# A hand-set order for the last layer's opening, attention stacks kept across layers, and a 128-row circuit network

## The chip, the cores and the metric

The kernel runs on one core of a Trainium2 chip. The core has five engines with queues of their own: TensorE (PE, matrix products, with weight loads shown as PEld), VectorE (DVE), ScalarE (ACT), GpSimd (POOL) and SyncE (SP, which here only issues DMAs). The metric is the device time in microseconds (us); smaller is better.

## What is computed

The input x has 2 batches of 1024 tokens with 128 features, in f32: 2048 tokens, worked as 16 tiles of 128 or 4 groups of 512 (groups 0 and 1 are the first batch). Four layers follow each other, each in this form:

```python
xn = layernorm(x)
x = x + attn(xn) * silu(ffn(xn))
```

- Layer 0: differential attention with 8 heads, and a ternary feed-forward network.
- Layer 1: attention in a window with 16 heads of 8, and 8 experts of which each token takes one.
- Layer 2: a "circuit": x1 = layernorm(xn + cumprod(cos(xn)) per head), q = cumprod(cos(first 16 features of x1)), then layernorm(x1 + W2 relu(W1 q + b1) + b2) with W1 512 x 16. As its ffn, 16 experts that each choose 256 tokens, beside one shared expert.
- Layer 3: causal attention with 16 heads of 8; as its ffn one linear layer whose 128 x 128 weight is rounded to 4 bits, plus a product of rank 16 (LoRA): xn Wq + (xn A) B + bias.

## The kernel before

x, xn, its transpose xnT and s (one of the two factors of the gating) stay in on-chip memory. The layers run one after the other.

**Attention of layers 1 and 3** is in the class `Heads`. `project_in(j)` makes the q and k products of one group (L527), splits each into three bf16 parts whose sum is the f32 number (`split3`, L464 to L467), and stores these to `parts` in DRAM (L541); then it makes the values into v (L548, L555). Heads are taken in fours, n = 0 to 7 (n // 4 is the batch). `loading_stacks(n)` gathers the parts of four heads as rows: a stack `ks` (L568) and a stack `qs` (L575), 12 DMAs on SP, in three buffers each (n % 3). Rows 72 to 127 of each stack are filled from a `blank` in DRAM (L512), once per layer, and v is set to ones (L501); in row 96 and on, q gets the negated row maxima (`maxima_rows`, L585 to L597), so that one product yields scores less their maximum.

In `l3_layer`, `maxima(n, c)` computes the scores of the c-th 512 tokens with 96 rows (sf L1674, sr L1689, with masks added by a product L1680) and reduces them on DVE (L1675, L1697). `attend(n, c)` computes them again transposed with 128 rows (st L1727), takes the exponential on ACT (L1736) and multiplies by v (o3p L647). `ahead(n)` loads stack n + 2 and makes the maxima of n + 1, and for n = 0, 1 projects groups 2 and 3. `Weave.run(main, side, a, b)` interleaves main with side, b steps of side to a steps of main; `later` defers a closure by some steps. In the loop over n only PE keeps the written order; in the opening none does, and the order of instructions is the scheduler's.

The opening runs: `enter` (layernorm and transposes; rs is made on POOL, L72) and `project_in` for groups 0 and 1, stacks 0, then groups 2 and 3, then `l3_ffn` for all groups (pz L1817, f3y L1822, and the 17-row LoRA and bias product L1823), then the maxima of n = 0, then the loop.

**Layer 2.** `Chosen.search` finds 16 thresholds in 15 rounds. `experts()` runs 97 steps, woven with `circuits()` and `forward()` (the circuit network). Per expert: weights (768 KB, L1574), gather of its tokens (POOL, L1536), transposes (L1541), f2g and f2u (L1497), gelu times product (L1499, L1501), f2y (L1583), scaling (L1593), and two scatters that add to `adds` in DRAM (POOL, L1556). `forward()` transposes q (L1445), makes h2p with 16 rows of contraction (L1454), relu (L1462), and y2p (L1470). At the end `adds` is fetched per group (L1630), passed through Silu (L1631) and gated into x on POOL (L148, L149).

Of the kernel before, what the change touches and what calls it, by code (L numbers as in the profile page):

```python
# [19 lines left out]
P = 128  # L20
# [26 lines left out]
BV = ("w3_s", "ln_g", "ln_b", "g1", "be1", "b2", "g2", "be2", "bv", "b2o")  # L47
WM = {}
for _n, _w in (
    ("qk1", 256), ("v1", 128), ("o1", 128), ("gate1", E1),  # L50
    ("w2_2", 512), ("gate2", E2), ("sh", 768),
    ("qk3", 256), ("v3", 128), ("o3", 128), ("kern", 128), ("lora_a", RANK),
):
    WM[_n] = (sum(w for _, w in WM.values()), _w)
# [88 lines left out]
def gate_residual(k, pool, t0, n, g, out=None, eng=None):  # L143
# [6 lines left out]
    if out is not None:  # L150
        nc.sync.dma_start(out[:, sl, :], k.x[:, sl, :])

# [260 lines left out]
def l0_ffn(k, wf):  # L413
    nc, tc = k.nc, k.tc
    w12, hw, w3 = wf
    with (
# [27 lines left out]
        for g in range(NG):  # L444
# [7 lines left out]
            y = tmp.tile([P, 4, D], F32, tag="y", name=f"f0y{g}")  # L452
# [8 lines left out]
def split3(k, pool, x, parts, n):  # L461

    nc = k.nc
    nc.scalar.copy(parts[0], x)  # L464
    nc.vector.tensor_tensor(x, x, parts[0], ALU.subtract)
    nc.scalar.copy(parts[1], x)
    nc.vector.tensor_tensor(parts[2], x, parts[1], ALU.subtract)  # L467


# [4 lines left out]
KD, KP, KM, KR = 72, 96, 99, P  # L474


class Heads:
# [5 lines left out]
    def __init__(self, k, ctx, weave, li, qk, v, o, bq=None, bk=None, bv=None, bo=None):  # L483
# [10 lines left out]
        self.dr = pool("d", 1, space=bass.MemoryType.DRAM)  # L494
        self.p_s, self.p_t, self.p_o = (pool("p" + n, c, space=PSUM) for n, c in (("s", 3), ("t", 3), ("o", 2)))

        self.ident_h = self.big.tile([P, P], BF16, tag="ident_h", name=f"ident_h{li}")
        nc.vector.tensor_copy(self.ident_h, k.ident)

        self.v = self.big.tile([P, NT, H1 * self.VW + 32], F32, tag="v", name=f"v{li}")  # L500
        nc.gpsimd.memset(self.v, 1.0)  # L501
# [5 lines left out]
        self.q, self.kk = [], []  # L507
        for j in range(3):
            q = self.big.tile([KR, 4, S], BF16, tag=f"qs{j}", name=f"qs{li}{j}")
            t = self.big.tile([KR, 4, S], BF16, tag=f"ks{j}", name=f"ks{li}{j}")  # L510
            for x in (t, q):
                nc.sync.dma_start(x[KD:P].rearrange("p h t -> p (h t)"), k.blank)  # L512
            self.q.append(q)
            self.kk.append(t)
        self.parts = [
            self.dr.tile([2, 3, P, S], BF16, tag=f"d{b}", name=f"parts{li}{b}") for b in range(B)
        ]

    def project_in(self, j):

        k, nc, u = self.k, self.k.nc, f"{self.li}{j}"
        b, c = divmod(j, 2)
# [1514 lines left out]
```

## Time and profile before

| what | value |
|---|---|
| runs before | 1928.09, 1928.19, 1936.4 us; median 1928.19 |
| profiled execution | 1931.13 us, span 1929.4 us, mean granted clock 0.926 |
| busy, share of the span | PE 88%, DVE 65%, ACT 44%, POOL 30% |

The stages in the profiled execution, by the span's clock:

| us | stage |
|---|---|
| 0 to 875 | layer 0's attention |
| 875 to 1036 | layer 0's feed-forward network |
| 1036 to 1087 | layer 1's opening, until its first exponentials |
| 1087 to 1285 | layer 1 |
| 1285 to 1388 | layer 2's opening, search and lists |
| 1388 to 1549 | layer 2's experts, until the last scatter is issued |
| 1549 to 1639 | last layer's opening |
| 1639 to 1929 | last layer's heads and the output |

A timeline line gives start, length, engine, line, operation, output <- inputs, shapes, how many, and in brackets the idle time before with what ended it. SPq is the issue of DMAs on SP's queue. The granted clock is 1 at full speed.

### The profile page before, as it was taken

The numbers are of one execution on the slowest core, as the hardware profiler recorded it, in microseconds if no ns is written. First come the engines' busy times: TensorE is split into PE (matmuls) and PEld (weight loads), VectorE is DVE, ScalarE is ACT, GpSimd is POOL, SyncE is SP. The second block draws the span as 40 slices with busy tenths as digits, with TensorE's granted clock in tenths as the row PEclk, the third lists the DMA queues.
The fourth block names the chain that finished last, engine by engine and source line by source line (L and its number), as shares of the span: only waits on it lengthen the run. The fifth ranks groups of instructions, "written<-read, shape, count | busy, mean of one in ns | idle before, by whom it ended". The sixth has DMA issues, their size and how long they took to land. (4 is left out here: it accounts for less than half of the span.)

```text
span 1929.4 us, 24564 instructions
## 1 busy us (share of the span) xinstructions
PE 1704.1 (88%) x7805; PEld 876.2 (45%) x7805; DVE 1255.6 (65%) x2572; ACT 845.4 (44%) x1850; POOL 571.9 (30%) x899
## 2 busy tenths in 40 slices
PE   4999999999999999989997698876589849999995
PEld 2344444444444444434445356444376724444442
DVE  3988888888878888863004454757671545887771
ACT  1555555555555555443114244342143330665564
POOL 2233333333334333330003622310164641102211
PEclk9999999999999999999998699986697965999998
DMA  6433333333424333330004554211042463112100
GB/s 193 100 89 84 89 81 101 84 93 78 101 71 105 79 88 81 74 87 0 1 0 100 123 144 125 65 61 27 24 127 70 95 136 54 43 43 56 32 2 12
DMA packets 111565, 145.58 MB, mean 75 GB/s; under 512 B 28019, under 2 KB 95740, under 8 KB 108204
## 3 DMA queue, kind: packets, MB, share of 16 engines
q1 hardware_dynamic: 85692, 93.12, 19.1%
q0 software_dynamic: 25456, 50.86, 10.8%
q8 instruction: 63, 1.03, 0.2%
q14 instruction: 66, 0.54, 0.1%
q10 hardware_dynamic: 288, 0.03, 0.0%
HBM read 60.22 MB, written 16.19 MB: 40 GB/s over the span
## 5 line engine op out<-in xcount | busy, mean ns | idle before, releaser
L281 PE MATMUL sc<-xnT,q 128*128 128x512 f32 x1024 | 506.2, 596 | 6.3 <-ACT e L293 6.3
L293 ACT ACTIVATE e<-sc,nm 128x1024 f32<-128x1024 f32 x256 | 285.2, 1114 | 350.2 <-DVE nm L291 267.5
L291 DVE TENSOR_REDUCE nm<-sc 128x1 f32<-128x1024 f32 x256 | 308.0, 1206 | 8.5 <-PE sc L281 8.4
L312 POOL DMA_DIRECT2D aT<-tT x384 | 205.0, 540 | 321.4 <-DVE tT L305 174.1
L281 PEld LDWEIGHTS sc<-xnT,q 128*128 128x128 f32 x1024 | 193.8, 191 | 234.3 <-issue 188.9
L323 PE MATMUL pz<-aT,xn 128*128 128x512 f32 x512 | 262.2, 596 | 4.8 <-DMA aT<-tT 4.8
L1736 ACT ACTIVATE e<-st 128x512 f32<-128x512 f32 (+3 forms) x384 | 166.2, 492 | 117.8 <-PE st L1727 111.8
L301 DVE SCALAR_TENSOR_TENSOR e<-e,c,e 128x1024 f32<-128x1024 f32 x128 | 164.1, 1282 | 3.3
L305 DVE STREAM_TRANSPOSE tT<-e 128x1024 f32<-128x1024 f32 x128 | 158.5, 1239 | 2.5 <-DMA aT<-tT 1.8
L323 PEld LDWEIGHTS pz<-aT,xn 128*128 128x128 f32 x512 | 97.9, 192 | 120.9 <-issue 112.0
L72 POOL TENSOR_TENSOR f<-fv,neg_half 128x1 f32<-128x1 f32 x128 | 83.8, 655 | 200.6 <-DVE fv L355 138.5
L1697 DVE TENSOR_REDUCE nm<-sr 128x1 f32<-128x384 f32 (+3 forms) x176 | 106.1, 637 | 38.1 <-PE sr L1689 37.6
L1727 PE MATMUL st<-qs,ks 128*128 128x512 bf16 (+3 forms) x384 | 116.2, 328 | 1.0 <-ACT e L1736 0.9
L341 PE MATMUL po<-vc,z 128*128 128x384 f32 x256 | 105.8, 495 | 5.8 <-ACT oc L352 2.2
L439 PE MATMUL f0h<-h,hw 128*128 128x512 f32 x256 | 110.0, 592 | 0.0
L1037 ACT ACTIVATE e<-st 128x384 f32<-128x384 f32 (+1 forms) x128 | 58.3, 476 | 115.9 <-PE st L1001 105.3
L1675 DVE TENSOR_REDUCE nf<-sf 128x1 f32<-128x512 f32 x128 | 82.2, 683 | 11.8 <-PE sf L1674 11.6
L647 PE MATMUL o3p<-e,v 128*32 128x512 f32 (+3 forms) x768 | 86.7, 498 | 0.0
L453 DVE TENSOR_TENSOR f0y<-f0o,bv 128x512 f32<-128x512 f32 x4 | 2.8, 692 | 121.3 <-PE f0o L449 121.3
L341 PEld LDWEIGHTS po<-vc,z 128*128 128x128 f32 x256 | 47.4, 191 | 72.8 <-issue 46.4
L439 PEld LDWEIGHTS f0h<-h,hw 128*128 128x128 f32 x256 | 48.6, 190 | 61.2 <-issue 61.2
L257 PE MATMUL pq<-xnT,m 128*128 128x512 f32 x128 | 69.6, 626 | 7.7 <-ACT oc L352 5.6
(381 smaller groups left out, 2606.3 us busy)
## 6 DMA issues: line engine op xcount, KB each, us to landing
aT<-tT SPq DMA_DIRECT2D x640, 64.0 KB
aT<-tT POOLq DMA_DIRECT2D x384, 64.0 KB
w<-in_l_e SPq DMA_DIRECT2D x16, 768.0 KB
qs<-parts SPq DMA_DIRECT2D x135, 64.0 KB
ks<-parts SPq DMA_DIRECT2D x45, 192.0 KB
parts<-hm SPq DMA_DIRECT2D x16, 384.0 KB
w<-in_l_w POOLq DMA_DIRECT2D x8, 640.0 KB
ks<-blank SPq DMA_DIRECT2D x6, 448.0 KB
```

The lines of the kernel that those rows point to most:

```text
L281: nc.tensor.matmul(ps[:, n * 512 : (n + 1) * 512], lhsT=q[:, m, hf * 512 + t * P : hf * 512 + (t + 1) * P], rhs=k.xnT[:, b * S + n * 512 : ...
L291: nc.vector.tensor_reduce(nm, ps, AX.X, ALU.max, negate=True)
L293: nc.scalar.activation(em, ps, AF.Exp, bias=nm, accum_out=(s1, s2)[m][:, t : t + 1])
L301: nc.vector.scalar_tensor_tensor(e[0], e[1], c, e[0], ALU.mult, ALU.add)
L305: nc.vector.transpose(tT[:, :, t % 2, :, :].rearrange("p j J c -> p J j c"), e[0].rearrange("p (J j a) -> p J j a", J=8, j=4),)
L312: (nc.gpsimd if j == 3 or (i == 0 and j > 0) else nc.sync).dma_start(aT[32 * j : 32 * j + 32, t - 1 : t + 1, i, :, :].rearrange("a t J c - ...
L323: nc.tensor.matmul(pz, lhsT=k.xn[:, 8 * b + J, :], rhs=st["aT"][:, :, :, J, :].rearrange("p t i c -> p (t i) c"), start=(J == 0), stop=(J ...
L341: nc.tensor.matmul(po.rearrange("p a d -> p (a d)"), lhsT=st["z"][:, t * P : (t + 1) * P], rhs=mats[h][1].rearrange("p a d -> p (a d)"), s ...
L439: nc.tensor.matmul(ph, lhsT=hw[:, l, c, j * P : (j + 1) * P], rhs=cur[:, c, cols], start=(c == 0), stop=(c == 3))
L1697: nc.vector.tensor_reduce(nm[:, tt, i0 : i0 + hb], ps, AX.X, ALU.max, negate=True)
L1727: nc.tensor.matmul(ps[:, n0:512], lhsT=kk[0:KR, i, kt * P : (kt + 1) * P], rhs=q[0:KR, i, c * 512 + n0 : c * 512 + 512], start=not diag, s ...
L1736: nc.scalar.activation(e[:, n0:512], ps[:, n0:512], AF.Exp)
```

## The change

- `Stacks` is made once, between layer 0's attention and its feed-forward network: the bf16 identity, v, the causal masks, the three pairs of stacks with their blank rows, and the parts in DRAM. Layers 1 and 3 share them. For layer 3 a stack is laid out as two halves of 512 tokens (`nc_` = 2), which can be loaded one by one.
- `project_in` is cut into `products`, `first_parts`, `split`, `store` and `project_values`. The first bf16 part is made straight from the product.
- Layer 3's opening is written out for PE, DVE, ACT, POOL and SP, and so is its loop: gating on DVE; groups 0 and 1; the first half of stack 0 on three queues; the maxima of the first 512 tokens; then attention for them, with the next maxima woven in. Groups 2 and 3 (`second_batch`) are woven into n = 1 and 2.
- Layer 3's rounded weight and its LoRA product are folded into one 128 x 128 matrix w3, in layer 2; the bias comes from a one-row product.
- The mask products of one tile in `maxima` become one.
- W1 of the circuit network is kept as four copies, padded with zeros to 128 rows; h2p takes 32 products of 256 columns for 16 of 512, in two halves.
- In the search, a step's candidate is made from a base prepared earlier.
- An expert's weights come in two DMAs (the f2y third behind the next expert's first part); some buffers are fewer (xg 3 for 4); the weave counts change.

```diff
+class Stacks:
...
+        nc.gpsimd.memset(self.v, 1.0)
...
+            for x in (t, q):
+                nc.sync.dma_start(x[KD:P], k.blank)
...
+        self.nc_, self.ct = (1, S) if li == 1 else (2, S // 2)
...
+            nc.scalar.activation(hm[:, 0, a, :], pq, **how)
+            if a == 1:
+                nc.scalar.activation(xf[:, 1, :], pq, **how)
+            elif bias is None:
+                nc.vector.tensor_scalar(xf[:, 0, :], pq, scale, None, ALU.mult)
+            else:
+                nc.vector.tensor_scalar(xf[:, 0, :], pq, scale, bias, ALU.mult, ALU.add)
...
+    def split(self, j):
+        nc = self.k.nc
+        xf, hm = self.hm[j]
+        for a in range(2):
+            nc.vector.tensor_tensor(xf[:, a, :], xf[:, a, :], hm[:, 0, a, :], ALU.subtract)
+            nc.scalar.copy(hm[:, 1, a, :], xf[:, a, :])
+        for a in range(2):
+            nc.vector.tensor_tensor(hm[:, 2, a, :], xf[:, a, :], hm[:, 1, a, :], ALU.subtract)
...
+            (nc.sync, eng or nc.sync)[a].dma_start(d[:, :, at : at + 512], self.hm[j][1][:, :, a, :])
...
-        eng, dma = (nc.vector, nc.sync) if self.li == 1 else (nc.gpsimd, nc.gpsimd)
+        eng, dma = (nc.vector, nc.sync) if self.li == 1 or n + c == 0 else (nc.gpsimd, nc.gpsimd)
...
+            if 0 < i < 14:
+                base = tile("base3", (P, 3), I32, bufs=2)
+                nc.vector.tensor_tensor(base, steps[:, i + 1, :], thr.to_broadcast([P, 3]), ALU.bitwise_or)
...
-                nc.vector.tensor_tensor(cand, steps[:, i + 1, :], thr.to_broadcast([P, 3]), ALU.bitwise_or)
+                nc.vector.tensor_tensor(cand, base, inc.to_broadcast([P, 3]), ALU.bitwise_or)
+        nc.vector.tensor_tensor(thr, thr, inc, ALU.bitwise_or)
...
+        w1 = pool.tile([P, 4, FF2], F32, tag="w1", name="w1_2")
+        nc.gpsimd.memset(w1, 0.0)
+        for i in range(4):
+            nc.gpsimd.dma_start(w1[32 * i : 32 * i + NQ, i, :], k.i["l2_w1"])
...
+            nc.tensor.matmul(pw, lhsT=k.lora[:, 0:P], rhs=k.lora[:, P:], start=True, stop=True)
+            nc.vector.tensor_tensor(k.w3, pw, wq, ALU.add)
...
-                    ph = [PS.tile([P, NG, P], F32, tag="y", name=f"h2p{i}_{j}") for i in (i0, i0 + 1)]
-                    for i in range(2):
-                        r = slice(32 * (i0 + i), 32 * (i0 + i) + NQ)
-                        nc.tensor.matmul(
-                            ph[i].rearrange("p n t -> p (n t)"),
-                            lhsT=k.w1_2[r, j * P : (j + 1) * P],
-                            rhs=qT[r, :, :].rearrange("p n t -> p (n t)"),
-                            start=True,
-                            stop=True,
-                        )
...
+                if n in (0, 2):
+                    h = gp.tile([P, 4, 4, 2, P], F32, tag="wide", name=f"h2{n}")
+                    for j in range(4):
+                        for i0 in (0, 2):
+                            ph = PS.tile([P, 2, 2, P], F32, tag="y", name=f"h2p{n}{i0}_{j}")
+                            for i in range(2):
+                                nc.tensor.matmul(
+                                    ph[:, i, :, :].rearrange("p n t -> p (n t)"),
+                                    lhsT=w1[:, i0 + i, j * P : (j + 1) * P],
+                                    rhs=qT[:, n : n + 2, :].rearrange("p n t -> p (n t)"),
+                                    start=True,
+                                    stop=True,
+                                )
+                            nc.scalar.activation(h[:, j, i0 : i0 + 2, :, :], ph, AF.Relu, bias=k.pv("b1", j))
+                            yield
...
-            weave.run(experts(), others, 1 + 6 * E2, 110)
...
+            weave.run(experts(), others, 1 + 6 * E2, 122)
...
-                    for i in range(hb):
-                        nc.tensor.matmul(
-                            ps[:, i, r - P : r],
-                            lhsT=hd.ident_h,
-                            rhs=mqk,
-                            start=(i == 0),
-                            stop=False,
-                            skip_group_check=True,
-                        )
+                    nc.tensor.matmul(
+                        ps[:, :, r - P : r],
+                        lhsT=hd.ident_h,
+                        rhs=mqk[:, None, :].to_broadcast([P, hb, P]),
+                        start=True,
+                        stop=False,
+                        skip_group_check=True,
+                    )
...
+        def gate(g):
+            nc.scalar.activation(z[g], z[g], AF.Silu)
+            gate_residual(k, hd.wk, 4 * g, 4, z[g], eng=nc.vector)
...
+            pt[g] = p_s.tile([P, 4, P], F32, tag="s", name=f"pt3{g}")
+            for i in range(4):
+                src, dst = k.x[:, 4 * g + i, :], k.xn[:, 4 * g + i, :]
+                if i % every:
+                    nc.vector.tensor_scalar(dst, src, m[:, i, 0:1], rs[:, i : i + 1], ALU.subtract, ALU.mult)
+                else:
+                    nc.scalar.activation(dst, src, AF.Identity, scale=rs[:, i : i + 1], bias=sh[:, i : i + 1])
+                nc.tensor.transpose(pt[g][:, i, :], dst, k.ident)
...
+        def linear(g):
+            py = p_s.tile([P, 4, D], F32, tag="s", name=f"f3y{g}")
+            nc.tensor.matmul(
+                py,
+                lhsT=k.ones[0:1, :],
+                rhs=k.bv("b3")[0:1, None, :].to_broadcast([1, 4, D]),
+                start=True,
+                stop=False,
+                skip_group_check=True,
+            )
+            for i in range(4):
+                t = 4 * g + i
+                nc.tensor.matmul(
+                    py[:, i, :],
+                    lhsT=k.xnT[:, t * P : (t + 1) * P],
+                    rhs=k.w3,
+                    start=False,
+                    stop=(i == 3),
+                    skip_group_check=True,
+                )
+            nc.scalar.activation(k.s[:, 4 * g : 4 * g + 4, :], py, AF.Silu)
...
+        def second_batch():
+            for g in (2, 3):
+                gate_residual(k, hd.wk, 4 * g, 4, z[g], eng=nc.vector)
+                yield
+                stats(g)
+                yield
+                norm(g, 1)
+                yield
+                turned(g)
+                yield
+                yield from hd.project_in(g)
+            for g in (2, 3):
+                linear(g)
+            yield
+        others = second_batch()
         def ahead(n):
-            if n + 2 < 8:
+            if n + 2 < 8 and n != 2:
                 hd.load_stacks(n + 2)
             if n + 1 < 8:
-                yield from maxima(n + 1, 0)
-                yield from maxima(n + 1, 1)
-            if n < 2:
-                yield from hd.project_in(2 + n)
+                for j, _ in enumerate(chain(maxima(n + 1, 0), maxima(n + 1, 1))):
+                    yield
+                    if n in (1, 2) and j % 5 == 4 and next(others, "end") != "end":
+                        yield
+            if n == 2:
+                for _ in others:
+                    yield
+                hd.load_stacks(n + 2)
...
+        with tc.manual_schedule(engines={E.PE, E.DVE, E.Activation, E.Pool, E.SP}):
+            for g in range(NG):
+                fetch(g)
+            warm = sp.tile([P, 1], F32, tag="warm", name="warm")
+            nc.scalar.activation(warm, k.half_pi, AF.Silu)
+            gate(0)
+            stats(0)
+            gate(1)
+            norm(0, 2)
+            turned(0)
+            hd.products(0)
+            stats(1)
+            norm(1, 2)
+            hd.first_parts(0)
+            turned(1)
+            hd.products(1)
+            hd.split(0)
+            hd.store(0, nc.gpsimd)
+            loads = hd.loading_stacks(0, None, slice(0, 1), (nc.sync, nc.gpsimd, nc.sync, nc.scalar))
+            hd.first_parts(1)
+            hd.project_values(0)
+            hd.split(1)
+            for _ in loads:
+                pass
+            hd.store(1, nc.gpsimd)
+            for _ in hd.loading_stacks(0, None, slice(1, 2), (nc.sync, nc.sync, nc.gpsimd)):
+                pass
+            hd.project_values(1)
+            linear(0)
+            linear(1)
+            for g in (2, 3):
+                nc.scalar.activation(z[g], z[g], AF.Silu)
+            weave.all(maxima(0, 0))
+            weave.flush()
+            hd.load_stacks(1)
+            def lead(gen, n):
+                for _ in range(n):
+                    next(gen)
+                    weave.tick()
+                return gen
+            o = [hd.wk.tile([P, 4, H1, DK], F32, tag="o", name=f"o3_0{c}") for c in range(2)]
+            weave.run(attend(0, 0, o[0]), maxima(0, 1), 16, 28)
+            m = lead(ahead(0), 10)
+            weave.run(attend(0, 1, o[1]), m, 32, 30)
+            for n in range(1, 8):
+                if n == 4:
+                    o = [hd.wk.tile([P, 4, H1, DK], F32, tag="o", name=f"o3_{n}{c}") for c in range(2)]
+                weave.run(both(n, o), ahead(n), 48, 42 + 8 * (n in (1, 2)))
...
+        l0_attention(k)
+        k.stacks = Stacks(k, ctx)
+        l0_ffn(k, (w12, hw, w3))
...
```

## The prediction

> **What bounds the kernel now.** I read the page's slices first, then the table of windows stage by stage, then the timelines of the two stretches where TensorE ran at half clock. Columns of the windows: length, then busy time of PE, PEld, DVE, ACT, POOL, then granted clock, DMA share, GB/s.
>
> ```profile
> 1445.00:1481.00 36.00, 35.26 (x109) 20.30 (x110) 4.75 (x11) 13.12 (x24) 13.26 (x11) 0.62 0.25 53
> 1481.00:1525.00 44.00, 44.00 (x307) 41.55 (x306) 22.10 (x62) 13.57 (x30) 29.67 (x24) 1.00 0.53 132
> 1525.00:1541.00 16.00, 11.36 (x73) 9.99 (x73) 9.54 (x24) 5.19 (x10) 7.89 (x6) 1.00 0.21 27
> 1541.00:1563.00 22.00, 0.40 (x4) 0.21 (x2) 6.48 (x21) 2.07 (x4) 16.12 (x16) 0.61 0.62 123
> 1563.00:1580.00 17.00, 11.77 (x45) 7.16 (x46) 12.58 (x37) 14.18 (x31) 6.65 (x6) 0.71 0.54 128
> 1580.00:1612.00 32.00, 30.12 (x79) 16.86 (x79) 4.46 (x11) 2.22 (x5) 1.03 (x2) 0.55 0.63 120
> 1612.00:1639.00 27.00, 24.08 (x93) 10.13 (x93) 23.10 (x42) 2.06 (x3) 3.93 (x13) 0.50 0.13 20
> 1639.00:1740.00 101.00, 100.62 (x812) 48.17 (x810) 82.32 (x148) 66.67 (x151) 12.98 (x37) 0.99 0.17 41
> ```
>
> See three things. The circuit network falls into 1445 to 1481, where PE is full but at clock 0.62. From 1541 to 1639 the last layer opens: 98 us in which PE is first idle (22 us), then busy at half clock with the layer's linear part (32 us), then paced by DVE's maxima (27 us). From 1639 the body is bound by PE at full clock, so work moved into it costs its full PE time. All else (layers 0 and 1, the search) is touched only at the edges.
>
> Timeline of PE in the network, then of the last layer's first steps on ACT, POOL, DVE, SP and PE (start, length, engine, line):
>
> ```profile
> 1458.91 2.08 PE L1454 MATMUL h2p<-q2T,w 16*128 16x512 f32 x4
> 1460.92 2.08 PE L1497 MATMUL f2u<-xT,w 128*128 128x256 f32 x4
> ...
> 1482.64 1.03 PE L1497 MATMUL f2u<-xT,w 128*128 128x256 f32 x4
> ```
> ```profile
> 1553.50 0.63 ACT L1631 ACTIVATE f2z<-f2z 128x512 f32<-128x512 f32 x1 [13.43 <-DMA f2z<-adds]
> 1554.77 2.48 POOL L148 TENSOR_TENSOR f2z<-f2z,s 128x512 f32<-128x512 f32 x2
> 1567.92 3.78 PE L527 MATMUL qp<-xnT,wm 128*128 128x512 f32 x4 [2.41 <-ACT xnT L65]
> 1574.55 1.98 PE L527 MATMUL qp<-xnT,wm 128*128 128x512 f32 x4 [0.87 <-ACT xnT L65]
> 1579.52 1.29 DVE L467 TENSOR_TENSOR hm<-xf,hm 128x512 bf16<-128x512 f32 x2
> 1582.84 0.29 SPq L575 DMA_DIRECT2D qs<-parts  x1
> 1584.04 1.12 SPq L568 DMA_DIRECT2D ks<-parts  x3
> 1638.58 0.63 PE L1727 MATMUL st<-qs,ks 128*128 128x512 bf16 x1
> ```
>
> The same 128-row product takes 3.78 us at half clock and 1.98 at full. The experts' f2u takes 2.08 beside the 16-row h2p and 1.03 after it.
>
> **The last layer.** I count T from the first Silu, 1553.50, on the profiled execution. Before, attention's stream of exponentials starts at 1638.58, T = 85.1.
>
> After, step by step for the first 512 tokens. Silu 0.63; gating on DVE, two operations of 0.69 (L465, the same shape) where POOL took two of 1.24 and was queued behind memsets; four pairs of statistics at 0.26 plus 0.15, with waits 1.4: T = 3.5. POOL's rs 1.04; DVE does the second group's gating beside it and ends at 4.9. The shift 0.17, two xn of 0.49 on ACT beside two on DVE, transposes, copy 0.56: T = 7.1. Products 3.78 at half clock: 10.9. ACT queues behind them: first parts 0.6 twice, xf 0.67, the next group's xnT 0.58, second parts 0.6 twice; DVE's last subtraction ends near 14.9. The stores: before, the last hm ended at 1580.81 and loads began at 1582.84 (q) and 1584.04 (k), so 2.0 to 3.2 us: T = 18. Loading: twelve full loads were issued over 7.3 us on SP (1582.84 to 1590.16); layer 1's needed 13.4 us from first issue (1057.26) to the first sr (1070.64). Half the bytes over three queues lie between 3.5 and 13.4; I take 7, nearest to the issue row: T = 25.
>
> Issuing: "DMA: Bandwidth & Descriptors", section on issuing engines, says that several issuers save only sequencer time on the same 16 engines. By that rule the spreading alone gives nothing and the halved bytes everything, some 6.7 instead of 7; no run here separates the two.
>
> PE meanwhile does the second products (2.0 to 3.8), values (twice 1.05 to 1.75) and two linear groups. A linear group is four 128-row matmuls, 0.37 each at full clock (half of the f3y pitch of 0.72 at clock 0.5), and a one-row bias over 512 columns, no such row here: between 0 and 1.9 (half of 3.78), taken as 1.0 from the 1.98 row. So 2.5 each, 5 at half clock; PE ends between T = 21.6 and 30. ACT's DMA issues stand behind its last second part (T near 20), and only its Silu of the linear part waits behind them.
>
> Maxima of the first 512 tokens: 6.1 (DVE, 1613.30 to 1619.35): 31.1. Four small DVE operations 0.8, transposes 0.6, nr 0.41, three row DMAs at 0.57 and landing: first st at T = 35.5, 50 us earlier than before. Beside attend(0,0) run the second 512 tokens' maxima, DVE-paced, 16.6 us before (1619.35 to 1635.95): 17, T = 52.5. Ten reductions of the next maxima lead, about 6, and cover POOL's row path (about 5): T = 58.5.
>
> The body: n = 3 starts at 1740.30 (its release of a stack on SP), so n = 0 to 2 take 101.7, 33.9 each, with two projections of 2.8 inside. At 0.22 per 512 bf16 columns (sr at 1644.21, the next matmul at 1644.43) a head costs attend 5.9 and 13.7, maxima 3.2 and 6.7, together 29.5; 8.9 of it, 30%, is already done. So the rest of n = 0 is 0.7 of (33.9 - 2.8) = 21.8 and n = 1 starts at T = 80.3, where before it started at 1672.5, T = 119.0: **38.7 ahead.** Given back in n = 1 and 2: one more projection 2.8, two linear groups 5.0, transposes 1.0, together 8.8. DVE gains some 6 us there (gating, statistics, xf) on 82 of 101: about 88%, hidden in PE's time. One new wait: stack 4 is loaded only at the end of ahead(2). In the order PE has some 10 us of work by columns, 12 by the body's pace, from the last split to the first use; before, stores at 1708.72 to loads issued by 1719.66 and 2 of landing took 13. A stall of 1 to 3 behind which DVE's and ACT's streams queue too; 1.5. Were the slack gone it would cost 13. **The last layer gains 38.7 - 8.8 - 1.5 = 28**, bounds 16 (loads at 13.4, linear at half clock) to 36.
>
> **The network.** Eight pairs of 16-row matmuls, 14.7 us in the trace, run two at a time: four records in 2.08 at half clock, 1.06 at full (1451.03). Padded to 128 rows nothing runs beside: the same columns cost 8 x 1.72 (pitch of the f2 passes, 0.215 per 256 columns) = 13.8 at full clock. The other 15.8 us of PE work from 1450.02 to 1480.55, mostly at half clock, are at full clock four f2 groups of 0.86, four f2y groups of 0.92, 0.87 of y2p and 0.33 of transposes, 8.3. So 30.5 becomes 22.1, **8 saved, if the clock stays full**; the 128-row stretch right after, equally full, has 1.00. If it does not: 8 x 3.78 = 30.2, 15.5 lost.
>
> The page "TensorE: Matmul & The Clock Gate", Part 1, lets the clock fall only after an idle window of about 3.4 us, and its table of goals says that a short contraction takes as long as a full one but runs beside others. By both, padding has no clock to win and loses the pairing: 15.5 slower. The trace disagrees with the first: 1458 to 1480 has no idle time and 0.50.
>
> Against it: POOL's order becomes scatter, gather, scatter, gather (1.85 + 1.3 each), and the next expert's scatter waits for the landing 4.15 after the second scatter's start (1541.28 to 1545.43): 7.3 per expert instead of 6.4, where the early experts came every 7.25; 1 us. The folded weight adds four PE steps and some 1.6 us of DVE before the network: 1 us. Net **6**, bounds -17 to 11.
>
> **The rest, taken as 0 within 4.** Blanks (2.7 MB), v's memset and masks go under layer 0's FFN (875 to 1036, DMA share 0.00, PE 96% busy); in layer 1 they had ended before the loads that its first sr awaited, and POOL's added work there costs about 2 on rs. In layer 2's opening POOL gets a memset of w1 and four DMAs of 0.57 ahead of rs, while DVE's statistics come sooner: minus 3 to plus 4. The search drops one operation of 0.2 from each chain round, and issues it elsewhere on a DVE that is 83% busy: 0 to 3 either way. Merged masks keep their columns.
>
> **Sum.** 28 + 6 = 34. Profiled execution 1931.1 (span 1929.4): 1897.1. The median of the runs lies 2.9 lower: **1894**.
>
> **Rivals.**
> 1. *The network stays at half clock* (16 rows were not the reason): 23.5 worse than forecast, 1917. For it: the dip at 1446 follows idle time. Against: f2u at 1.03 as soon as h2p ends. Chance 0.12.
> 2. *The second batch binds the body*: each DVE wait in the written order stops PE, stack 4 is late by 13 and linear runs at half clock; about 16 worse, 1910. For it: PE has no slack there. Chance 0.16.
> 3. *More is won*: the whole 36 us at 0.62 become full (13.7), loads land at T = 21, layer 2 opens 3 earlier: 1880. Chance 0.11.
> 4. *Slower: PE stays at half clock when attention starts thinly fed.* Each microsecond of full-speed work costs one more; the gain of 34 is eaten after 34 us of such work, and two heads of it (some 52) give 1946. Before, the clock rose within 3 us of the first dense st (1638.58 to 1641.5), which speaks against it. Chance 0.04.
> 5. *It doesn't do what it says*: the opening's steps wait for the same stores and stacks as before and only the linear part's removal counts, given back in the body: about 1925. Chance 0.02.
>
> The forecast has 0.55. The range, **1877 to 1914**, leaves out half of rival 1, rivals 4 and 5 and tails. Half a per cent, 9.6 us, is about what a measurement of this kernel tells from no change: under 1918.5 is faster (forecast, 2, 3, most of 1: 0.88), over 1937.8 slower (0.04), between 0.08.
>
> **What would show it.** Right: h2p at clock 1.0 with 30 us become 22; the first st 34 to 37 us after the first Silu; stacks loaded 6 to 8 us after their first issue; n = 3 about 28 us earlier relative to that Silu; under 3 us of PE idle at stack 4. Wrong: PE windows at 0.5 after the first st, PE waiting on DVE in n = 1 and 2, or f2 passes still at 0.5 us beside h2p.

## The result, and the profile after

The change makes the kernel faster by 1.36%: ratio 0.9864 (95% interval 0.9835 to 0.9893), 1904.01 us median of 4 runs (1902.94 to 1908.33) beside 1929.82 us of the kernel before on the same chip. The forecast was 1894 us, 10 us too low, inside its range. The profiled execution took 1908.33 us (span 1906.6, mean granted clock 0.941). A second profile of the same kernel, taken with the experiments (label after2), has a span of 1901.3.

The spans, cut at the same events in every trace (us):

| stretch | before | after | after2 | forecast of the difference |
|---|---|---|---|---|
| start to layer 1's first masked maximum (sr) | 1070.6 | 1069.8 | 1068.3 | rest: 0 within 4 |
| layer 1's first to its last sr | 193.0 | 186.9 | 184.5 | rest |
| to the search's first product (pc) | 56.0 | 51.6 | 50.2 | rest |
| to the first scatter | 90.8 | 88.8 | 88.8 | rest |
| to the last layer's first Silu | 143.0 | 152.0 | 152.7 | -6 |
| to the end | 375.9 | 357.5 | 356.8 | -28 |
| sum | 1929.4 | 1906.6 | 1901.3 | -34 |

(The rows are rounded; the sums are the spans.) So three terms were off, and they partly cancel: the last layer won 18.4 instead of 28, the experts' stretch lost 9.0 instead of winning 6, and "the rest" won 13.4 in this pair of profiles (the table's first four rows), where nothing was expected. That the total came within 10 us is luck: 24.6 us of misses stood against 13.4 us of gains that were not forecast.

The last layer's windows after, columns as in the prediction's windows. The rows follow the opening: projections and loads, first maxima, attention and maxima of the first heads, the rest of n = 0, n = 1 and 2, n = 3.

```profile
1555.40:1574.70 19.30, 15.76 (x53) 8.50 (x54) 10.19 (x24) 11.00 (x20) 4.31 (x6) 0.71 0.30 95
1574.70:1586.30 11.60, 5.90 (x31) 2.84 (x32) 7.25 (x16) 0.92 (x1) 2.04 (x4) 0.58 0.29 83
1586.30:1610.80 24.50, 21.34 (x138) 9.66 (x139) 22.34 (x41) 6.88 (x16) 2.35 (x7) 0.92 0.48 97
1610.80:1632.30 21.50, 21.33 (x153) 9.05 (x156) 17.52 (x31) 14.18 (x31) 2.34 (x7) 1.00 0.01 2
1632.30:1720.40 88.10, 79.89 (x572) 37.25 (x576) 65.88 (x132) 56.36 (x121) 12.41 (x31) 0.98 0.20 46
1720.40:1756.20 35.80, 34.16 (x274) 16.40 (x275) 26.62 (x48) 21.57 (x50) 7.11 (x16) 1.00 0.21 42
```

The fifth row is the one to look at: PE is idle for 8.2 of 88.1 us. The same two steps, n = 1 and 2, in the kernel before:

```profile
1672.50:1740.30 67.80, 67.54 (x566) 32.45 (x559) 56.68 (x104) 45.08 (x105) 8.74 (x24) 1.00 0.25 60
```

They took 67.8 us there, with 0.3 us idle: n = 1 and 2 give back 20.3 us.

The first masked maximum and the first attention product of the last layer in the trace after, with what PE waited for:

```profile
1549.10 0.63 ACT L1825 ACTIVATE f2z<-f2z 128x512 f32<-128x512 f32 x1 [12.67 <-DMA f2z<-adds]
1574.71 0.38 PE L1750 MATMUL sr<-ks,qs 96*128 96x128 bf16 x4 [1.84 <-DMA qs<-parts]
1586.32 0.58 PE L1788 MATMUL st<-qs,ks 128*128 128x512 bf16 x1 [3.35 <-DMA qs<-nr]
```

Counted from the first Silu at 1549.10, sr comes at T = 25.6 (forecast 25) and st at T = 37.2 (forecast 35.5). The first load of the half stacks was issued at 1567.90, so sr came 6.8 us later (forecast 7). The opening does what it was said to do.

### The profile page after: what moved, and what is told of

Read it like the earlier page. It is cut to its first block, busy times and chain, and to the rows that moved or that the text cites. A ratio compares the mean times of both kernels' runs of the same rounds, so it can differ in the third digit from the quotient of the medians.

```text
span 1906.6 us, 24480 instructions
## 1 busy us (share of the span) xinstructions
PE 1675.6 (88%) x7703; PEld 870.1 (46%) x7727; DVE 1257.5 (66%) x2597; ACT 850.9 (45%) x1849; POOL 561.7 (29%) x888
## 4 chain that ended last, share of the span: by engine, by line
PE 52%; DVE 21%; DMA 8%; ACT 6%; POOL 5%; issue 5%; SPq 2%; POOLq 0%; DVEq 0%; ACTq 0%
PE sc L292 10%; PE f0h L450 6%; PE pz L334 5%; DVE nm L302 5%; DMA aT<-tT 4%; PE o3p L699 4%; DVE tT L316 3%; DVE e L312 3%; PE st L1788 2%; PE po L352 2%; ACT e L304 2%; PE pq L268 2%; POOL aT L323 2%; SPq L323 2%; DVE nm L1758 2%
## 5 line engine op out<-in xcount | busy, mean ns | idle before, releaser
L1788 PE MATMUL st<-qs,ks 128*128 128x512 bf16 (+3 forms) x360 | 108.2, 324 | 6.9 <-DMA qs<-nr 4.0
```

The source lines that it names most:

```text
L1788: nc.tensor.matmul(ps[:, n0:512], lhsT=kk[0:KR, kt // 4, i, kt % 4 * P : (kt % 4 + 1) * P], rhs=q[0:KR, c, i, n0:512], start=not diag, sto ...
```

## The experiments

All times are ratios to the kernel before on the same chip, with 95% intervals, and stretches of one profile each, cut as in the table above. Line numbers shift a little from kernel to kernel.

**The experts' stretch.** Two things changed there: the network's few-row products, and the experts' row buffers (4 became 3, which I had priced at 1 us).

xg4, the changed kernel with four buffers again:

```diff
-                    xg[ex] = hp.tile([P, 2, D + E2], F32, tag="xg", name=f"xg{ex}", bufs=3)
+                    xg[ex] = hp.tile([P, 2, D + E2], F32, tag="xg", name=f"xg{ex}", bufs=4)
```

> The changed kernel with four buffers for the experts' gathered rows (xg) instead of three; nothing else. Theory A (the third buffer binds): with three, the gather for expert ex+2 stands on POOL behind ex-1's scaled rows, and TensorE waits for the landing (12.1 us of waits xgt <- xg between 1397 and 1445). With four, POOL's order is gather, gather, scatter, scatter, those waits fall under 3 us, the scatters of the first six experts come every 7.0 to 7.6 us instead of 9.5, and the first Silu of the last layer comes 8 to 10 us earlier: about 1895 us beside 1904. Theory B (the weave's new counts or the network's work bind, not the rows): scatters stay 9 to 10 us apart and the time is within 3 us of the changed kernel's.

Measured: 1890.87 us, ratio 0.9820 (0.9798 to 0.9842); the stretch from first scatter to first Silu is 138.9 us instead of 152.0 and 152.7, 13 to 14 us shorter where 8 to 10 were expected. POOL's timeline, first in the changed kernel, then in xg4:

```profile
1405.71 1.58 POOL L1633 DMA_INDIRECT adds<-ye,idx  x1 [2.09 <-DVE sh L97]
1407.60 0.99 POOL L1622 DMA_INDIRECT xg<-rows,idx  x1 [0.30 <-PE f2g L1582]
1408.89 1.57 POOL L1633 DMA_INDIRECT adds<-ye,idx  x1 [0.31 <-issue]
1410.77 0.99 POOL L1622 DMA_INDIRECT xg<-rows,idx  x1 [0.30 <-issue]
```
```profile
1397.15 1.61 POOL L1633 DMA_INDIRECT adds<-ye,idx  x1 [0.63 <-DVE ye L1671]
1399.07 1.54 POOL L1633 DMA_INDIRECT adds<-ye,idx  x1 [0.30 <-issue]
1400.91 1.01 POOL L1622 DMA_INDIRECT xg<-rows,idx  x1 [0.31 <-issue]
1403.21 1.01 POOL L1622 DMA_INDIRECT xg<-rows,idx  x1 [0.20 <-issue]
```

What ended most of PE's idle time in the changed kernel from 1397 to 1445 (us in total, times, longest), and in xg4 from 1390 to 1432, where gathered rows are not among the waits:

```profile
PE xgt L1627 <- DMA xg<-rows,idx: 12.1, 6, 3.4
```
```profile
PE f2g L1582 <- ACT xT L1629: 5.8, 2, 3.7
PE amT L1504 <- DVE am L1502: 2.7, 1, 2.7
```

The 12.1 us of waits for gathered rows are gone; theory A. Its detail on POOL's order was wrong: the pairs are scatter, scatter, gather, gather, as before. Part of its price stays as other waits: the first scatters of the first six experts come 8.2 us apart in the mean (1390.00 to 1430.81), where the changed kernel has 9.5 (1397.08 to 1444.82) and I expected 7.0 to 7.6.

bxg3, the kernel before with three buffers (the same edit the other way round).

> The kernel before with three xg buffers instead of four; nothing else. Theory A (the third buffer binds): POOL's order becomes scatter, gather, scatter, gather; the early experts' scatters go from 7.25 us apart to about 9.5, and the time rises by 5 to 9 us, to 1935 to 1939. Theory B (the order costs next to nothing, as my prediction put it: about 1 us): within 2 us of 1930.

Measured: 1948.79 us, ratio 1.0115 (1.009 to 1.014), the stretch 164.5 us instead of 143.0, or 21.4 us more. PE waits 15.5 us for xg between 1404 and 1454, where the kernel before has no such wait. Theory A, at more than twice the 5 to 9 us that it was given.

h16, the changed kernel with 16-row products:

```diff
-                                    lhsT=w1[:, i0 + i, j * P : (j + 1) * P],
-                                    rhs=qT[:, n : n + 2, :].rearrange("p n t -> p (n t)"),
+                                    lhsT=w1[r, i0 + i, j * P : (j + 1) * P],
+                                    rhs=qT[r, n : n + 2, :].rearrange("p n t -> p (n t)"),
```

with r the 16 rows of i0 + i, and the two products in two PSUM tiles with an activation each (these lines are left out).

> The changed kernel with the network's first matmuls over 16 rows again, two to two PSUM tiles, 256 columns each as in the change; the padded weight stays, and its 16 activations of 512 columns a half become 32 of 256. Theory A (the few rows pull the clock down): granted clock 0.5 to 0.7 while they run, against 1.00 in the changed kernel, the experts' f2 passes beside them at about 0.5 us a record pitch instead of 0.25; but since the experts wait for gathered rows there, only part of the lost 8 us is seen: 3 to 8 us slower, 1907 to 1912. Theory B (the clock was low for another reason, the idle time ahead): clock 0.95 or more with 16 rows too, and the time within 2 us.

Measured: 1918.66 us, ratio 0.9961 (0.9941 to 0.9981); the stretch 162.5 us, 10 more than the changed kernel's 152.0 and 152.7. The whole is 18 to 19 us slower by the ratios, more than the 3 to 8 expected. The profiled execution was the shortest of its 12, and where the other 8 us lie no profile shows. Windows of 4 us in h16 from where 16-row products of the second half begin, then the changed kernel's in its second half:

```profile
1476.00:1480.00 4.00, 4.00 (x21) 2.24 (x21) 1.86 (x7) 2.37 (x7) 2.68 (x3) 1.00 0.18 41
1480.00:1484.00 4.00, 3.44 (x12) 1.90 (x12) 0.00 (x0) 2.32 (x5) 3.39 (x3) 0.74 0.65 148
1484.00:1488.00 4.00, 4.00 (x17) 2.79 (x16) 0.69 (x1) 0.84 (x2) 0.15 (x1) 0.50 0.09 22
1488.00:1492.00 4.00, 4.00 (x18) 2.62 (x15) 0.61 (x2) 1.07 (x3) 0.75 (x1) 0.50 0.06 12
```
```profile
1486.00:1490.00 4.00, 4.00 (x20) 3.54 (x19) 0.69 (x1) 2.55 (x4) 3.39 (x3) 1.00 0.71 166
1490.00:1494.00 4.00, 4.00 (x28) 3.74 (x27) 0.90 (x2) 1.48 (x3) 1.51 (x2) 1.00 0.28 35
```

PE is nearly full in both, but with 16 rows the clock drops to 0.50 and stays there until these products end (1.00 again from 1500). The longest idle piece in the first four windows is 0.56 us, and the same wait of 1.28 us for gathered rows stands shortly ahead of both stretches (until 1475.33 and 1483.01). Theory A.

b128, the kernel before with the padded weight alone:

```diff
-                            lhsT=k.w1_2[r, j * P : (j + 1) * P],
-                            rhs=qT[r, :, :].rearrange("p n t -> p (n t)"),
+                            lhsT=w1[:, i0 + i, j * P : (j + 1) * P],
+                            rhs=qT.rearrange("p n t -> p (n t)"),
...
```

(The lines that build w1 in layer 2 are left out.)

> The kernel before with the padded 128-row weight of the network alone (built in layer 2, as in the change); four xg buffers stay. Theory A (clock): the windows of the network go from clock 0.62 to 1.00, the 30.5 us from 1450 to 1480.5 become about 22, and nothing else binds: 6 to 8 us faster, about 1923. Theory B (the padding only undoes the pairing): clock as before, up to 15 us slower. Theory C (the gather chain binds there too): clock 1.00 but under 3 us won.

Measured: 1916.27 us, ratio 0.9944 (0.9922 to 0.9966); the stretch 134.4 us instead of 143.0. Its window of the network and two products in it:

```profile
1448.00:1467.90 19.90, 19.90 (x73) 11.43 (x72) 2.23 (x5) 11.76 (x18) 7.75 (x7) 1.00 0.28 65
```
```profile
1460.82 1.88 PE L1454 MATMUL h2p<-q2T,w 128*128 128x512 f32 x4
1462.54 1.03 PE L1497 MATMUL f2u<-xT,w 128*128 128x256 f32 x4
```

Theory A: clock 1.00 and 8.6 us won in the stretch, and some 11 us in the whole, more than the 6 to 8 expected. The 30.5 us of the network (1450.02 to 1480.55 before) are 22.1 here (1447.44 to 1469.52), as forecast. The page "TensorE: Matmul & The Clock Gate" of the Trainium skill, Part 1, names an idle window of about 3.4 us as what brings half clock back. h16 differs from it, with half clock behind idle pieces of 1.28 us and less, and the measurement decides.

**Layers 1 and 2 ahead of the experts.** oldsplit is the changed kernel with layer 1's projections split in the old way (its order, per half: ACT copies, DVE subtracts, ACT copies, DVE subtracts):

```diff
         self.products(j)
+        if self.li == 1:
+            yield from self.old_parts(j)
+            self.project_values(j)
+            yield
+            return
         self.first_parts(j)
...
```

(The body of `old_parts` is left out.)

> The changed kernel with layer 1's projections split as before: ACT and DVE each copy a product to xf first, then first part on ACT, subtraction on DVE, second part on ACT, subtraction on DVE, one half after the other; the last layer keeps the new split. Theory A (the new split is what made layer 1's body shorter: DVE no longer stands in front of the maxima with subtractions that wait for ACT): the stretch from layer 1's first to its last masked maximum goes from 181 to 187 us in the three traces of changed kernels back to 190 to 193, and the time rises by 6 to 9 us, to about 1912. Theory B (the blanks and the fill of v, now done under layer 0, made it shorter): the stretch stays under 187 and the time within 2 us.

Measured: 1913.05 us, ratio 0.9929 (0.9915 to 0.9943); layer 1's stretch 189.8 us, where nine kernels with the new split have 180.2 to 187.2 (mean 183.5) and the kernel before and its three variants 189.8 to 193.1 (mean 191.6). What PE's sr products waited for on DVE in layer 1's first 80 us, in the kernel before, in oldsplit and in after2:

```profile
PE sr L963 <- DVE nr L595: 2.5, 1, 2.5
PE sr L963 <- DVE v L552: 2.3, 1, 2.3
```
```profile
PE sr L1033 <- DVE nr L670: 2.5, 1, 2.5
PE sr L1033 <- DVE v L631: 2.3, 1, 2.3
```
```profile
PE sr L1009 <- DVE nr L646: 0.4, 1, 0.4
```

And the windows from 1110 of the same three kernels:

```profile
1110.00:1120.00 10.00, 10.00 (x97) 5.23 (x93) 5.13 (x13) 3.14 (x7) 2.52 (x5) 0.72 0.83 236
```
```profile
1110.00:1120.00 10.00, 10.00 (x95) 5.27 (x95) 5.21 (x12) 2.98 (x7) 2.09 (x3) 0.70 0.67 200
```
```profile
1110.00:1120.00 10.00, 9.76 (x115) 6.43 (x114) 6.21 (x17) 3.91 (x8) 5.08 (x7) 1.00 0.84 197
```

The old split brings back the same two waits to a tenth of a microsecond, and after each of them a window at a clock of 0.70 to 0.86. In front of v and of the row copy nr stand DVE's subtractions, which wait for ACT. First the kernel before, whose subtractions alternate with ACT's copies, then after2, where they come in pairs:

```profile
1104.57 0.69 DVE L465 TENSOR_TENSOR xf<-xf,hm 128x512 f32<-128x512 f32 x1 [1.10 <-ACT hm L464]
1105.94 0.69 DVE L467 TENSOR_TENSOR hm<-xf,hm 128x512 bf16<-128x512 f32 x1 [0.68 <-ACT hm L466]
1107.92 0.69 DVE L467 TENSOR_TENSOR hm<-xf,hm 128x512 bf16<-128x512 f32 x1 [0.69 <-ACT hm L466]
```
```profile
1102.83 1.29 DVE L588 TENSOR_TENSOR hm<-xf,hm 128x512 bf16<-128x512 f32 x2 [0.57 <-ACT hm L586]
```

DVE waits 2.5 us for ACT there and 0.6 us here; v and nr follow all four subtractions in both. Theory A: 6.3 of the 8.1 us between the two means, by one trace of oldsplit. By the ratios the whole lost 12 us, more than the 6 to 9 expected; beside after2 the trace has 3.0 us more ahead of layer 1's first sr and 3.0 more in the last layer, which no run explains.

unshare, the changed kernel with `Stacks` made inside each attention layer:

```diff
-        k.stacks = Stacks(k, ctx)
         l0_ffn(k, (w12, hw, w3))
...
-        hd = Heads(k, ctx, weave, 1, "qk1", "v1", "o1")
+        k.stacks = Stacks(k, ctx); hd = Heads(k, ctx, weave, 1, "qk1", "v1", "o1")
...
-        weave = Weave()
+        weave = Weave(); k.stacks = Stacks(k, ctx)
```

> The changed kernel with the stacks, values and masks made by each attention layer again, from pools of its own; the written orders and the new split stay. Theory A (with the layer's own pools, layer 2's first tiles lie where layer 1's stacks lay, and its statistics are put behind layer 1's end): from layer 1's last masked maximum to the search's first product 55 to 56 us again instead of 50 to 52, 4 to 5 us slower, and layer 1's body stays short. Theory B (the earlier statistics come from elsewhere in the change): 50 to 52 us. For the last layer: its blanks and fills come back before its first maxima; if they cost, first Silu to first st grows from 37 us by 1 to 5. Time 1905 to 1914 by A, 1902 to 1908 by B.

Measured: 1916.77 us, ratio 0.9948 (0.993 to 0.9965). Layer 2 opens in 52.5 us, close to theory B's 50 to 52 and far from A's 55 to 56: sharing is not what made it open early. But the stretch to the first Silu grows to 168.8 us, 16 more. Its last 25 us in the windows, and what SP issued there:

```profile
1530.00:1555.00 25.00, 0.00 (x0) 0.00 (x0) 2.44 (x1) 1.20 (x1) 4.74 (x5) 0.50 0.81 153
```
```profile
1536.31 0.62 SPq L505 DMA_DIRECT2D qs<-blank  x1
1537.05 10.66 SPq L1822 DMA_DIRECT2D f2z<-adds  x4
```

The blanks are loaded here, from 1534.13 on, and in the written order of SP the load of the experts' sums stands behind them. So with this order the sharing is worth 16 us; I had looked for that cost behind the first Silu (sr at T = 25.7, unchanged).

bfirst followed: the kernel before with only layer 2's pool of small tiles made ahead of its other pools.

```diff
+        tc.tile_pool(name="l2t", bufs=2) as tmp,
         tc.tile_pool(name="l2", bufs=1) as pool,
...
-        tc.tile_pool(name="l2t", bufs=2) as tmp,
```

> The kernel before with one thing changed: layer 2's pool of small tiles (statistics among them) is made first among layer 2's pools, so that its tiles lie elsewhere in SBUF. Theory A (layer 2's statistics stood behind layer 1's end because their tiles lay where ACT and DVE still worked for layer 1): DVE takes them ahead of the last output projection's copies; from layer 1's last masked maximum to the search's first product 51 to 53 us instead of 56.0, and the time falls by 3 to 5 us, to 1922 to 1924. Theory B (the place in memory sets the order but something else ends the opening): 55 to 56 us, no change of time.

Measured: 1924.61 us, ratio 0.9975 (0.9961 to 0.999); layer 2 opens in 49.8 us instead of 56.0. DVE in the kernel before, then in bfirst:

```profile
1291.25 0.68 DVE L902 SCALAR_TENSOR_TENSOR xnT<-xnT,s 128x512 f32<-128x512 f32 x1
1291.85 0.29 DVE L83 BATCH_NORM_STATS2 st<-x 128x6 f32<-128x128 f32 x1
```
```profile
1281.47 0.49 DVE L83 BATCH_NORM_STATS2 st<-x 128x6 f32<-128x128 f32 x2
1285.17 0.66 DVE L638 COPY s<-yp 128x512 f32<-128x512 f32 x1
```

Before, the first statistics follow layer 1's last copies; with another place in memory they are taken ahead of them. Theory A. In the changed kernel too the first statistics stand ahead of these copies (1279.67 and 1281.27). There the sizes of layer 2's pools differ, which places these tiles anew; that this is what moved them is likely, and not shown.

**The last layer.** loadsp issues the first half stacks' twelve loads on SP alone:

```diff
-            loads = hd.loading_stacks(0, None, slice(0, 1), (nc.sync, nc.gpsimd, nc.sync, nc.scalar))
+            loads = hd.loading_stacks(0, nc.sync, slice(0, 1))
```

> The changed kernel with the first half stacks' twelve loads all issued by SP instead of by SP, POOL and ACT in turn; the halved bytes stay. Theory A (the issuing on one queue is what ends last): twelve issues at 0.61 are 7.3 us and landing 2 more, so the first masked maximum comes 2 to 4 us later than 25.6 us after the first Silu (25.3 mean), and the whole 2 to 4 us longer, about 1907. Theory B (the bytes on the shared engines end last, and several issuers save nothing): within 0.7 us of 25.3, time within 2 us of 1904.

Measured: 1904.97 us, ratio 0.9857 (0.9835 to 0.9879), beside 0.9865 (0.9844 to 0.9885) of after2; sr at T = 25.9 instead of 25.4. From the first issue to sr it takes 7.1 us (1567.27 to 1574.39) instead of 6.8. SP's queue shows why it costs so little: nine q loads in 3.07 us, 0.34 each, where I had reckoned 0.61.

```profile
1567.27 1.13 SPq L628 DMA_DIRECT2D ks<-parts  x3
1568.50 3.07 SPq L628 DMA_DIRECT2D qs<-parts  x9
```

The 0.61 was no issue time: in the kernel before, an issue of a q load took 0.26 to 0.30 us as well, but SP also waited three times, 2.5 us in all, for earlier loads to land. Theory B in so far as the spreading buys half a microsecond at most; that the halved bytes did the rest fits, since here SP has no such wait, but no run loads full stacks in the new opening. The page "DMA: Bandwidth & Descriptors" of the Trainium skill, section "Issuing engines are not separate DMA queues", says that DMAs run on the same engines whoever issues them and that several issuers save only issue time; this run agrees, with its 0.5 us.

sb1 (on xg4) spreads the second batch's steps: every fourth step of the maxima, transposes a step behind the rows that ACT makes.

```diff
-                    if n in (1, 2) and j % 5 == 4 and next(others, "end") != "end":
+                    if n in (1, 2) and j % 4 == 3 and next(others, "end") != "end":
...
```

> The changed kernel with four xg buffers, and in the last layer the second batch's steps spread wider in n = 1 and 2: one every fourth step of the maxima instead of every fifth, the transposes a step after the normalised rows that ACT makes, and each linear group by itself. Theory A (of the 88 us that n = 1 and 2 take, 8 are TensorE waits for ACT and DVE behind this written order, which the spacing caused): waits of TensorE in n = 1 and 2 fall from 8 to under 4 us, no half-clock slices, first Silu to the end 3 to 6 us shorter than the 355.6 us of the kernel with four xg buffers alone: about 1886. Theory B (DVE and ACT are simply short of time there): same waits at other places, within 2 us of 1891.

Measured: 1890.23 us, ratio 0.9796 (0.9774 to 0.9818); first Silu to the end 357.6 us, not shorter than xg4's 355.8. PE's waits in n = 1 and 2 add up to 7.3 us instead of 7.6. They moved, as theory B said: the wait for xn is gone, others came.

sb2 (on xg4) takes the second batch's gating, statistics, normalised rows and transposes out of n = 1 and 2 into the opening:

```diff
...
+            gate_residual(k, hd.wk, 8, 4, z[2], eng=nc.vector)
+            stats(2)
             weave.all(maxima(0, 0))
             weave.flush()
+            norm(2, 1)
+            turn(2)
+            turned(2)
+            gate_residual(k, hd.wk, 12, 4, z[3], eng=nc.vector)
+            stats(3)
+            norm(3, 1)
...
```

and the last transposes behind the ten leading reductions of n = 0.

> As the run with four xg buffers, but the second batch's gating, statistics, normalised rows and transposes stand in the last layer's opening, where DVE waits 3.7 us for the first stacks and 4.2 us for the first row maxima; only its projections and linear part stay in n = 1 and 2. Theory A: 2.6 us of transposes and 3 to 5 us of waits leave the stretch that TensorE bounds, at a cost of 0 to 2 us in the opening: first Silu to the end 4 to 8 us shorter than 355.6: about 1885. Theory B (DVE's steps in the opening delay the first maxima and row path one to one): the first st comes 3 to 6 us later than 37 us after the first Silu, and nothing is won: 1888 to 1894.

Measured: 1881.1 us, ratio 0.9754 (0.9739 to 0.9769), the fastest version here, 1.1% under the changed kernel, of which the fourth buffer gives about 0.5 (xg4). First Silu to the end is 348.9 us; the first st stays at T = 37.3, so the work in the opening costs nothing up to there, and 0.9 us until n = 1 begins (T = 84.1 beside 83.2). n = 1 and 2 in sb2, and its PE waits there:

```profile
1616.00:1695.80 79.80, 75.80 (x574) 36.02 (x572) 59.90 (x109) 54.33 (x113) 11.55 (x35) 1.00 0.21 51
```
```profile
PE o3p L699 <- ACT e L1797: 1.4, 1, 1.4
PE st L1785 <- ACT e L1797: 0.7, 3, 0.3
PE nmT L644 <- DVE nm L1758: 0.5, 1, 0.5
```

The changed kernel's three largest waits in its 88.1 us, for comparison:

```profile
PE pt L1848 <- ACT xn L1847: 2.8, 2, 1.6
PE nmT L644 <- POOL n L639: 1.0, 1, 1.0
PE sf L1736 <- DVE nm L1758: 0.8, 1, 0.8
```

79.8 us instead of 88.1, waits 3.9 instead of 7.4 in all. Theory A.

best is sb2 with the projections at every ninth step and both linear groups in one, so that ACT loads its tables twice instead of four times.

```diff
-                    if n in (1, 2) and j % 5 == 4 and next(others, "end") != "end":
+                    if n in (1, 2) and j % 9 == 8 and next(others, "end") != "end":
...
```

> As the kernel with four xg buffers and the second batch's gating to transposes in the opening, but its projections at every ninth step of the maxima instead of every fifth, and both linear groups in one step, so that ACT loads its tables twice instead of four times (1.28 us each). Theory A (ACT and DVE bunch up where the projections stand close): TensorE's waits in n = 1 and 2 fall from 3.9 to under 2.5 us and first Silu to the end from 348.9 to 345 to 348: about 1878. Theory B: the waits move and the time stays within 2 us of 1881.

Measured: 1886.52 us, ratio 0.9777 (0.9756 to 0.9798); first Silu to the end 351.8 us, n = 1 and 2 80.5 us. Not better than sb2; if anything worse, though the intervals overlap. The waits only moved (4.5 us in all), as in theory B, but its "within 2 us of 1881" missed by 3.5; what the wider spacing cost is open.

after2, the changed kernel once more.

> The changed kernel itself once more, as a base on the same chip for the other runs of this set. Its first profile had layer 1 from first to last masked maximum at 186.9 us, five of its variants with the same layer 1 at 180.3 to 183.6: theory A (the first profile was a slow draw) expects 181 to 184 here and a median of 1900 to 1904; theory B (the variants change it) 186 to 188.

Measured: 1903.48 us, ratio 0.9865 (0.9844 to 0.9885); layer 1 at 184.5 us. The median is theory A's, the stretch lies between the two ranges: layer 1's stretch varies by some 3 us to either side from profile to profile, which bounds what the rows on layer 1 can tell.

## Why the prediction was right, and where it was wrong

**What bounds the kernel now.** Right: the half-clock network and the 98 us opening were where the change acts. Wrong in one sentence: that all else is touched "only at the edges".

**The last layer, 28 forecast, 18.4 measured.**
- The opening, step by step: sr at T = 25.6 (25), first st at 37.2 (35.5), attend(0,1) at 61.8 (58.5), n = 1 at 83.2 (80.3). Of the 1.7 us by which st was late, 0.6 came ahead of sr, 0.6 in the maxima and 0.5 on the row DMAs, which SP issued from 1583.23 and for which st waited 3.35 us. n = 1 began 35.8 us ahead instead of 38.7. The 7 us taken for the loads came out as 6.8, in part by luck: the issue row of 7.3 that they were set by held SP's waits.
- Failed step: "Given back in n = 1 and 2 ... together 8.8", with DVE's 6 us "hidden in PE's time". The added work was about right: transposes 2.6, the two linear groups 4.4, one projection 1.8 and its values 1.1, together 9.9 us. But PE also stood idle for 8.2 us where it had stood 0.3, in waits of 0.2 to 1.6 us, most of them for ACT and DVE, and behind the longest of these waits the clock fell (0.83 in the slice from 1642 to 1652), which belongs to the last 2.5 (10 us at 0.83 lose 1.7, an estimate). That is 20.3, not 10.3, and n = 3 came 15.5 us earlier against the first Silu instead of 28. PE's waits in n = 1 and 2 were among the prediction's own signs of being wrong. DVE was 75% busy there (65.9 of 88.1) and still did not hide its work, with the order in which PE waits for it fixed by hand. sb1 and sb2 tell the cause apart: spreading the steps moved the waits, taking work out of the stretch ended half of them.
- The new wait for stack 4 (1.5) did not come; loads were issued from 1707.99 and n = 3 began at 1720.4 without a wait for them.
- Some 2.9 us came back after n = 3 (186.2 instead of 189.1, all of it behind the last heads, 40.1 instead of 43.4). No run shows why.

**The network and the experts, 6 won forecast, 9.0 lost measured.**
- "8 saved, if the clock stays full": right, 8.6 (b128) and about 10 (h16) in the stretch, and by way of the clock as forecast.
- Failed step: "POOL's order becomes scatter, gather, scatter, gather ... 1 us". It cost some 11.5 us in the changed kernel (xg4 and its three followers 138.9 to 141.3, mean 140.4, against 150.1 to 152.9, mean 151.9, in the changed kernel's two profiles, loadsp and oldsplit) and 21.4 in the kernel before. I priced POOL's issue and the scatters' landing and left out what the gather brings. With three buffers the gather for expert ex+2 waits for the scaled rows of ex-1, which read the gate from the same buffer. In the trace after, f2y ends at 1412.8, the scatter starts at 1415.29, the second gather is issued at 1420.40, and the transposes that need it run at 1423.66: 10.9 us, in which PE has one expert's work and then waits. With four buffers there is one expert more between.

```profile
1423.66 0.47 PE L1627 MATMUL xgt<-ident,xg 128*128 128x128 f32 x1 [2.42 <-DMA xg<-rows,idx]
```

- "The folded weight ... 1 us": not separated. Four-buffer kernels with everything else take 140.4 us and b128 134.4; the 6 us between them hold the folded weight, the split into halves and the new counts of the weave.

**The rest, 0 within 4 forecast, 13.4 and 18.6 won measured.** Failed step: layer 1 was looked at for blanks and POOL's fills only. The new split sits in `Heads`, which both layers use, and it took 4.8 us of waits (0.4 is left in after2) and the stretches of lower clock after them out of layer 1 (oldsplit). Layer 2's opening won 4.4 to 5.8, outside the bound of 3; the reason (bfirst) was not among those I listed. Of the 2.0 us between the search's first product and the first scatter no run shows the cause. The blanks were held to be free under layer 0, and that held (1069.8 and 1068.3 us until layer 1's first sr, beside 1070.6); what they would have cost elsewhere shows in unshare.

**Rivals.** Rival 1 (clock stays low) fell. Rival 2 (the second batch binds the body) is what happened in part: its price was 16, the stretch lost 10 more than forecast, by waits on ACT as much as on DVE, without a wait for stack 4 and with the linear groups at full clock. Rival 3 fell on balance, though its layer 2 term came. Rivals 4 and 5 fell: clock 0.92 from the first st on, 1.00 after.

## What to carry to other kernels

A buffer count is a latency budget: before one buffer fewer is called free, follow its reuse loop (last reader, queue, issue, landing, first use) and compare it with the work of one turn, not with the issue times alone. A helper that two layers share changes both, so look at every caller's waits; and moving work under an engine with spare time pays only if nothing waits for it in a fixed order, so put it where that engine and its waiters are both idle. Where a new layer's first tiles lie in memory can set when the layer starts.

## What was not expected of the hardware

- A PE that was busy in 4.00 of 4.00 us ran at clock 0.50 with 16-row products among its work (h16, 1484 to 1492) and at 1.00 with the same products padded to 128 rows (changed kernel, 1486 to 1494). From 1476 to 1492 no idle piece of h16 was longer than 0.56 us.
- ACT's table load took 1.28 us each time that Silu and Exp took turns; sb2 has four of them in n = 1 and 2, best two.
- Twelve loads for half a stack left SP in 4.2 us (1.13 and 3.07), while the full stacks' twelve had taken 7.3 (1582.84 to 1590.16 in the kernel before). The issues themselves were alike (0.26 to 0.30 us for most q loads of either); the difference is what SP waited between them.
